# A graph-attention layer and a graph-convolution layer on one core: the projection by seven half-size products, the bias seeded in PSUM, layer 0's statistics split between two engines, and one written list of steps

## The chip, the core and the metric

One NeuronCore of a Trainium2 chip runs one program. TensorE (PE) multiplies into PSUM; VectorE (DVE), ScalarE (ACT) and GpSimd (POOL) work on rows of 128 partitions; SyncE (SP) issues most transfers, and POOL issues those whose row numbers come from a table in SBUF. Each engine takes its instructions in their written order and waits on semaphores of the others. The metric is the device time of one execution in microseconds (us); lower is better. One run of this kernel differs from another by about 0.3% (2322.24 to 2328.84 us in three runs).

## The reference

The input x has 32 batches of 512 channels by 1024 nodes; adj is 512 by 512.

```
layer 0:  q = wq . x[b],  k = wk . x[b]            (one number a node)
          scores[m, n] = leaky(q[n] + k[m]),  att = softmax over n
          agg = x[b] att^T,  out = relu(adj agg + bm)
          x = layernorm(x + out)                   (over the 1024 nodes)
layer 1:  W = adj * adj,  out[m, f] = sum_n W[n, m] x[n, f] + bias[f]
          x = layernorm(x + out)
```

The kernel never builds the 1024 by 1024 attention matrix. The score depends on q[n] + k[m] alone, so with the nodes sorted by q the softmax sums become prefix sums. Both kernels project first, z = adj x, together with q, k and a column of ones (514 columns a node), put these rows in order of q, make tables of prefix sums, and take for each node three rows of a table.

## The kernel before

**Roles.** Four batches are in work at a time. In "slot" s of the main part (`slot`, s = 1 to 29) batch s is in layer 0's end and layer 1, `mid` = s+1 has its tables made and its rows fetched, `new` = s+2 is projected and ranked, and `old` = s-1 is normalised and stored. `begin` and `opening` fill this pipeline and `end` empties it. `tc.manual_schedule()` keeps every engine's instructions in the order in which the Python code issues them, so the order of work is the order of the calls in `slot` and `phase`.

**Projection of `new`** (`project`, L266 to L282): for each of 8 groups of 128 nodes, 4 channel blocks by 2 halves of the 514 columns, 64 matmuls of 128x257 in fp32. The trace shows two MATMUL records for one fp32 matmul. `keep` (L260) copies a group's PSUM tile to `zrow` on ACT.

**Ranking of `new`.** `spread` transposes q into every partition (`qb`), `place` (L324, DVE, 1024 elements) counts for each node how many q are smaller, `send` (L338, POOL, an indirect transfer) writes the node's row of `zrow` to that place of a DRAM table `td` (two such tables alternate), and after the eighth `send` `fetch` (L377, SP, eight transfers) reads the sorted rows back into `zs`: its first six bring blocks 8, 0, 1 and 7 (424 rows of 2056 bytes), the last two the rest.

**Tables of `mid`, one slot later.** `weigh` (L395) makes the factors `lq` for four of the nine blocks of `zs` (part 0) and for the others (part 1): Exp on ACT, products on DVE. `table` (L424) runs nine steps; each is four matmuls, a copy out on ACT, a carried row copied by POOL and one by ACT, and two stores of rows to `td`. `pick` (L450, POOL, indirect) then fetches three table rows for each node, eight transfers of 128 x 6168 bytes.

**Batch s.** `shares`, `scale` and `gain` weight and add the three rows. `turn` transposes into PSUM and ACT writes relu(. + bm) into y. `add` adds x (DVE). Layer 0's statistics are `stats` (two bn_stats and one bn_aggr a row block, DVE), `root` (POOL), `shift` (DVE) and `apply` (ACT). Layer 1 is already a product by seven half-size products: `sums` makes T1 to T4 (eight half rows of 128x512), `layer1`'s `make` multiplies, 28 matmuls of 128x512, and `read` (L613 to L617) adds the seven products up from PSUM on DVE, 18 reads of 128x512, the first ones onto a bias held in SBUF. `phase` writes the order of the last 26 us of a slot: reads, places, sends and picks alternate, and `fetch(new)` is followed on POOL's queue by one more pick.

PSUM has eight banks: three two-bank tiles rotate under the tag "mm", one under "t".

Of the kernel before, what the change touches and what calls it, by code (L numbers as in the profile page):

```python
# [23 lines left out]
def gat_gcn_resnorm_kernel(  # L24
# [11 lines left out]

# [8 lines left out]
    ZW = C + 2  # L79
    G = P // 2  # L80
# [8 lines left out]
    xpool = ctx.enter_context(tc.tile_pool(name="xpool", bufs=12))  # L89
    tpool = ctx.enter_context(tc.tile_pool(name="tpool", bufs=3))  # L90
    ypool = ctx.enter_context(tc.tile_pool(name="ypool", bufs=4))
    vpool = ctx.enter_context(tc.tile_pool(name="vpool", bufs=4))
    junk = ctx.enter_context(tc.tile_pool(name="junk", bufs=1))
    small = ctx.enter_context(tc.tile_pool(name="small", bufs=3))
    single = ctx.enter_context(tc.tile_pool(name="single", bufs=1))
    ps_mm = ctx.enter_context(tc.tile_pool(name="ps_mm", bufs=3, space=bass.MemoryType.PSUM))
    ps_t = ctx.enter_context(tc.tile_pool(name="ps_t", bufs=1, space=bass.MemoryType.PSUM))
# [11 lines left out]
    vec = const.tile([3 * CT, P], F32, name="vec")  # L109
# [4 lines left out]
    bm_sb = const.tile([P, CT], F32, name="bm_sb")  # L114
    bias_bc = const.tile([P, N], F32, name="bias_bc")


# [34 lines left out]
    zs = const.tile([P, NB, ZW], F32, name="zs")  # L152
# [6 lines left out]
    xs = {}  # L159
    kept = {}  # L160

    def load(b, ct):
        xt = xpool.tile([P, N], F32, name=f"x_{b}_{ct}", tag="x")
        nc.sync.dma_start(out=xt, in_=x[b, ct * P : (ct + 1) * P, :])
        xs.setdefault(b, []).append(xt)

    for b in range(3):
        for ct in range(CT):
            load(b, ct)
        if b == 0:  # L170
            nc.sync.dma_start(out=bias_bc, in_=bias.partition_broadcast(P))
# [4 lines left out]
    for td in tdb:  # L176
        nc.sync.dma_start(
            out=td.rearrange("(s u) c -> s u c", u=3)[N:NS, 0, :], in_=zs[P + N - NS : P, 0, :]
        )
        odd = td.rearrange("(s w u) c -> s w (u c)", w=2, u=3)  # L180
        for r in range(0, NS // 2, P):
            n = min(P, NS // 2 - r)
            nc.sync.dma_start(
                out=odd[r : r + n, 1, ZW : 3 * ZW],
                in_=zs[0:n, 0:2, :].rearrange("p j c -> p (j c)"),
            )


    wmT = const.tile([P, CT, ZW], F32, name="wmT")
    w1 = adj_sb  # L190

    def turn_weights():
        pt = ps_t.tile([P, N], F32, name="pt_v", tag="t")
        nc.tensor.transpose(pt[:, 0 : 3 * CT], vec, ident[0 : 3 * CT, 0 : 3 * CT])
        nc.vector.tensor_copy(wmT[:, :, 0], pt[:, 0:CT])
        nc.vector.tensor_copy(wmT[:, :, C + 1], pt[:, CT : 2 * CT])
        nc.vector.tensor_copy(bm_sb, pt[:, 2 * CT : 3 * CT])
        for ct in range(CT):
            pt = ps_mm.tile([P, C], F32, name=f"pt_{ct}", tag="mm")
            for ot in range(CT):  # L200
                nc.tensor.transpose(
                    pt[:, ot * P : (ot + 1) * P], adj_sb[:, ot, ct * P : (ct + 1) * P], ident
                )
            if ct % 2:
                nc.scalar.copy(wmT[:, ct, 1 : C + 1], pt)
            else:
                nc.vector.tensor_copy(wmT[:, ct, 1 : C + 1], pt)
# [7 lines left out]
    def square_weights():  # L215


        nc.vector.tensor_tensor(w1, adj_sb, adj_sb, ALU.mult)
        for ct in range(CT):
            nc.vector.tensor_tensor(  # L220
                w1[:, ct, ct * P : (ct + 1) * P], w1[:, ct, ct * P : (ct + 1) * P], ident, ALU.add
            )
# [4 lines left out]
        nc.vector.tensor_tensor(bias_bc[:, hi], bias_bc[:, hi], bias_bc[:, lo], ALU.subtract)  # L227
# [11 lines left out]
    room = {  # L239
        ("T1", 0): (5, 2), ("T2", 0): (5, 0), ("T2", 1): (5, 1),  # L240
        ("T1", 1): (6, 0), ("T3", 1): (6, 2), ("T3", 0): (6, 1),
        ("T4", 0): (7, 0), ("T4", 1): (7, 2),
    }

    info = {}
    ys = {}
    vs = {}
    ranks = {}
    due = {}
    us = {}  # L250
    ops = {}
    zps = {}
    tabs = {}
    tds = {}
    mixes = {}
    bws = {}
    qbs = {}
    tops = {}

    def keep(b, nt):  # L260

        nc.scalar.copy(  # L262
            zrow[:, nt, :].rearrange("p (h c) -> p h c", h=2), zps.pop((b, nt))[:, :, 0:CE]
        )

    def project(b, nt, part, kept=True):  # L266

        xb = xs[b]
        if part == 0:
            zps[b, nt] = ps_mm.tile([P, 2, H], F32, name=f"zp_{b}_{nt}", tag="mm")  # L270
        zp = zps[b, nt]
        for ct in range(part * CT // 2, (part + 1) * CT // 2):
            for h in range(2):
                nc.tensor.matmul(  # L274
                    zp[:, h, 0:CE],
                    xb[ct][:, nt * P : (nt + 1) * P],
                    wmT[:, ct, h * CE : (h + 1) * CE],
                    start=(ct == 0),
                    stop=(ct == CT - 1),
                )  # L280
        if part == 1 and kept:
            keep(b, nt)  # L282

    def peak(b):
# [3 lines left out]
        kc = small.tile([P, NT], F32, name=f"kc_{b}", tag="kc")  # L288
        nc.vector.tensor_copy(kc, zrow[:, :, C + 1])
        nc.vector.memset(zrow[:, :, C + 1], 1.0)  # L290
        info[b] = kc

    def spread(b, to="lq"):

        pool, tag = (ps_mm, "mm") if to == "v" else (ps_t, "t")
        qb = pool.tile([P, N], F32, name=f"qb_{b}", tag=tag)
# [4 lines left out]
        mx = ps_mm.tile([P, N], F32, name=f"mx_{b}", tag="mm")  # L301
        nc.tensor.transpose(mx[:, 0:P], tops.pop(b).to_broadcast([P, P]), ident)
        qmax = small.tile([P, 1], F32, name=f"qmax_{b}", tag="qmax")
        bw = small.tile([P, 2], F32, name=f"bw_{b}", tag="bw")
        nc.vector.tensor_reduce(qmax, mx[:, 0:P], AX.X, ALU.max)
        nc.vector.tensor_scalar(bw, nel, qmax, None, ALU.mult)
        if to == "v":
            qs = vpool.tile([P, N], F32, name=f"qs_{b}", tag="v")
            nc.scalar.copy(qs, qb)
            qb = qs  # L310
        else:
            qs = lq[:, 0:N]
            nc.scalar.copy(qs, qb)
        td = tdb[b % 2]
        rank = single.tile([P, NT], F32, name=f"rank_{b}", tag="rank")
        ranki = single.tile([P, NT], U32, name=f"ranki_{b}", tag="ranki")
        sgn = single.tile([P, NT], F32, name=f"sgn_{b}", tag="sgn")
        ranks[b] = (rank, ranki)
        tds[b] = td
        bws[b] = bw  # L320
        info[b] = (qs, info[b], sgn, qmax)
        qbs[b] = qb

    def place(b, *some):  # L324

        rank, ranki = ranks[b]
        qs = qbs[b]
        for nt in some:
            o = N - P - nt * P
            lt = junk.tile([P, N], I8, name=f"lt_{b}_{nt}", tag="lt")  # L330
            nc.vector.scalar_tensor_tensor(  # L331
                lt, qs, zrow[:, nt, 0:1], first[:, o : o + N],
                ALU.subtract, ALU.is_lt, accum_out=rank[:, nt : nt + 1],
            )
        n0, n1 = some[0], some[-1] + 1
        nc.vector.tensor_scalar(ranki[:, n0:n1], rank[:, n0:n1], 3.0, None, ALU.mult)  # L336
# [723 lines left out]
```

## Time and profile before

| what | value |
|---|---|
| median of 3 runs | 2324.92 us (2322.24, 2328.84, 2324.92) |
| span of the profiled execution | 2323.5 us; the page gives no time outside it |
| mean granted TensorE clock | 0.978 |
| busy PE / DVE / ACT / POOL | 2206.9 / 2003.3 / 1403.0 / 1042.8 us |
| from 0 to the first slot | 184.56 us |
| 29 slots | 1997.34 us, 68.87 us each |
| after the last slot | 141.60 us |
| moved by DMA | 548.68 MB |

How to read it: the span is that of one execution. A group row gives the line, the engine, the operation, out<-in, shape and count, then the total busy time, the mean of one instruction in ns, and the idle time before. A timeline row begins with start and length in us; a bracket at its end is the idle time before it and who ended it. Where rows run back to back their lengths overlap, so that the distance of starts, not the length, is the cost of one in a stream.

### The profile page before, as it was taken

What the parts mean: (1) busy time and instruction counts of PE and PEld (TensorE: products, weight loads), DVE (VectorE), ACT (ScalarE), POOL (GpSimd) and SP (SyncE); (2) the same over time, 40 slices, a digit from 0 to 9 for tenths busy, and PEclk for the clock granted to TensorE, in tenths of its full rate; (3) what the DMA queues carried; (4) which work ended last, traced back from release to release, by engine and by line L of the source; (5) the groups of instructions that cost most, each with busy time, mean ns of one, the idle gap of its engine ahead of it and who ended that gap; (6) DMA issues with size and microseconds to landing.
All of it is one profiled execution on the core that took longest, in us unless ns stands there. A gap on an engine that the chain in (4) does not pass through costs nothing.

```text
span 2323.5 us, 30952 instructions
## 1 busy us (share of the span) xinstructions
PE 2206.9 (95%) x9521; PEld 1388.3 (60%) x9521; DVE 2003.3 (86%) x4153; ACT 1403.0 (60%) x2185; POOL 1042.8 (45%) x1296
## 2 busy tenths in 40 slices
PE   8969999999999999999999999999999999999775
PEld 7636666566665656666656665656666665666332
DVE  4278989888998988899988898998899888889777
ACT  2665566666556667566667556666656666755543
POOL 2424444544444544444453444454444454444433
PEclk9979999999999999999999999999999999999877
DMA  6657878777878777787877787877777877777741
GB/s 250 200 165 238 261 239 280 245 222 235 252 242 265 257 230 231 241 263 248 270 238 220 239 257 240 274 257 224 227 248 253 260 257 231 227 239 248 235 164 73
DMA packets 175421, 548.68 MB, mean 236 GB/s; under 512 B 24748, under 2 KB 24760, under 8 KB 175256
## 3 DMA queue, kind: packets, MB, share of 16 engines
q1 hardware_dynamic: 117888, 277.18, 40.3%
q0 software_dynamic: 57344, 269.52, 33.2%
q8 instruction: 76, 1.25, 0.2%
q14 instruction: 89, 0.73, 0.1%
q10 hardware_dynamic: 24, 0.01, 0.0%
HBM read 338.17 MB, written 208.43 MB: 235 GB/s over the span
## 4 chain that ended last, share of the span: by engine, by line
DVE 42%; DMA 19%; PE 16%; issue 7%; POOL 6%; ACT 6%; SPq 2%; POOLq 0%; DVEq 0%; ACTq 0%
DVE lt L331 12%; DVE v L617 9%; DMA zs<-td 8%; PE zp L274 8%; DVE st L515 6%; PE tp L431 5%; DMA td<-zrow,ranki 5%; DMA rows<-td,idx 4%; DVE rows L589 4%; DVE rows L506 3%; DVE y L553 2%; POOL td L341 2%; PE op L544 2%; DMA td<-ts 2%; SPq L389 2%
## 5 line engine op out<-in xcount | busy, mean ns | idle before, releaser
L274 PE MATMUL zp<-wmT,x 128*128 128x257 f32 x4096 | 947.7, 383 | 1.4 <-ACT zrow L262 1.3
L274 PEld LDWEIGHTS zp<-wmT,x 128*128 128x128 f32 x4096 | 757.5, 190 | 163.4 <-issue 36.8
L440 POOL COPY zs<-ts 1x513 f32<-1x513 f32 x251 | 191.2, 762 | 676.3 <-ACT ts L436 675.3
L431 PE MATMUL tp<-zs,lq 128*64 128x257 f32 x2304 | 333.2, 404 | 63.5 <-DVE lq L411 24.8
L506 DVE SCALAR_TENSOR_TENSOR rows<-rows,ra 128x512 f32<-128x512 f32 x512 | 379.4, 762 | 11.7 <-ACT rows L498 2.5
L452 POOL DMA_INDIRECT rows<-td,idx x256 | 291.9, 1140 | 204.0 <-issue 115.8
L341 POOL DMA_INDIRECT td<-zrow,ranki x256 | 279.0, 1090 | 119.7 <-DVE ranki L336 46.6
L331 DVE SCALAR_TENSOR_TENSOR lt<-qb,zrow,first 128x1024 int8<-128x1024 f32 x240 | 307.1, 1280 | 4.3
L474 ACT ACTIVATE ac<-s 128x4 f32<-128x4 f32 x64 | 13.3, 208 | 486.4 <-DVE s L473 387.9
L431 PEld LDWEIGHTS tp<-zs,lq 128*64 128x64 f32 x2304 | 153.3, 140 | 224.6 <-POOL zs L440 82.5
L356 ACT ACTIVATE sg<-lq,kc 128x1024 int8<-128x1024 f32 x240 | 275.1, 1146 | 6.8
L605 PE MATMUL oA<-y,adj_sb 128*128 128x512 f32 x512 | 243.8, 609 | 11.0 <-ACT y L536 9.9
L436 ACT COPY ts<-tp 128x514 f32<-128x514 f32 x288 | 168.4, 585 | 110.5 <-PE tp L431 85.5
L605 PE MATMUL oS<-rows,ws 128*128 128x512 f32 x480 | 210.9, 591 | 0.0
L498 ACT ACTIVATE rows<-rows,ra 128x512 f32<-128x512 f32 x256 | 166.8, 711 | 55.7 <-DVE ra L485 50.2
L262 ACT COPY zrow<-zp 128x514 f32<-128x514 f32 x256 | 144.8, 577 | 84.1 <-PE zp L274 76.6
L523 POOL TENSOR_SCALAR rs<-mv 128x1 f32<-128x1 f32 x256 | 88.6, 346 | 237.7 <-DVE mv L517 140.6
L553 DVE TENSOR_TENSOR y<-y,x 128x1024 f32<-128x1024 f32 x128 | 156.1, 1219 | 45.1 <-ACT y L548 45.1
L536 ACT ACTIVATE y<-y,nb,rs 128x1024 f32<-128x1024 f32 x128 | 158.5, 1238 | 54.5 <-DVE nb L530 53.2
L524 POOL TENSOR_TENSOR rs<-rs,mhalf 128x1 f32<-128x1 f32 x256 | 180.4, 705 | 21.4
L515 DVE BATCH_NORM_STATS2 st<-y 128x6 f32<-128x512 f32 x256 | 163.8, 681 | 2.7 <-issue 0.2
L605 PEld LDWEIGHTS oA<-y,adj_sb 128*128 128x128 f32 x512 | 94.1, 195 | 120.5 <-issue 98.1
(119 smaller groups left out, 2640.5 us busy)
## 6 DMA issues: line engine op xcount, KB each, us to landing
x<-in_x_dram SPq DMA_DIRECT2D x128, 512.0 KB
out_dram<-v SPq DMA_DIRECT2D x126, 512.0 KB
td<-ts SPq DMA_DIRECT2D x512, 120.5 KB
zs<-td SPq DMA_DIRECT2D x64, 602.3 KB
zs<-td SPq DMA_DIRECT2D x64, 240.9 KB
zs<-td SPq DMA_DIRECT2D x96, 120.5 KB
td<-ts SPq DMA_DIRECT2D x64, 96.4 KB
td<-zs SPq DMA_DIRECT2D x8, 514.0 KB
```

The source lines that it names most:

```text
L274: nc.tensor.matmul(zp[:, h, 0:CE], xb[ct][:, nt * P : (nt + 1) * P], wmT[:, ct, h * CE : (h + 1) * CE], start=(ct == 0), stop=(ct == CT - 1),)
L331: nc.vector.scalar_tensor_tensor(lt, qs, zrow[:, nt, 0:1], first[:, o : o + N], ALU.subtract, ALU.is_lt, accum_out=rank[:, nt : nt + 1],)
L341: sc = nc.gpsimd.indirect_dma_start(out=td[:, :], out_offset=bass.IndirectOffsetOnAxis(ap=ranki[:, nt : nt + 1], axis=0), in_=zrow[:, nt, ...
L356: nc.scalar.activation(sg, qs, AF.Sign, bias=kc[:, nt : nt + 1], accum_out=sgn[:, nt : nt + 1])
L431: nc.tensor.matmul(tp[i * G : (i + 1) * G, h, 0:CE], lw[:, ks[i], :], zs[:, j, h * CE : (h + 1) * CE], start=True, stop=True,)
L440: by.tensor_copy(zs[0:1, to, 1:ZW], ts[0:1, 1:ZW])
L452: nc.gpsimd.indirect_dma_start(out=rows[:, mt, :], out_offset=None, in_=tds[b].rearrange("(s u) c -> s (u c)", u=3), in_offset=bass.Indire ...
L506: nc.vector.scalar_tensor_tensor(u, g[:, k, i, 1 : C + 1], ra[:, k, i : i + 1], u, ALU.mult, ALU.add)
L515: nc.vector.bn_stats(st[:, h, :], t[:, h * H : (h + 1) * H])
L553: nc.vector.tensor_tensor(t, t, xs[b][ot], ALU.add)
L605: nc.tensor.matmul(ops[b, w][:, m, :], quarters[w][:, a, m * P : (m + 1) * P], part(y, a), start=(a == 0), stop=(a == CT // 2 - 1),)
L617: by.tensor_tensor(vs[b, mt][:, half], x0, x1, ALU.add)
```

## The change

The kernel is largely rewritten; what a batch computes is the same.

- **Projection by seven products.** Nodes by channels by columns are split in halves; four sums of quarters of x (`mix`, DVE, 128x512 each) are made for each of two groups of node blocks. 14 pairs of half products, 56 matmuls of 128x257, run into three PSUM tiles of fixed name A, B, C. Partial results are read in the middle of an accumulation (`keep`): eight copies of 128x514 on ACT and six additions of 128x514 on DVE.
- **Layer 1.** The bias is written into PSUM by `seed` before the products (four bf16 matmuls of 128x512 with a matrix of ones, the bias as three bf16 parts). The products accumulate in PSUM; four reads of 128x1024 are copies on ACT and three are additions on DVE. T1 to T4 are four subtractions of 128x1024. `SC` = 32 scales W and with it layer 1's sum.
- **Layer 0's statistics.** ACT's relu is gone: `add` takes max(PSUM, -bm) + x in one DVE instruction and takes the row's sum along. `square` makes the mean (ACT, one column) and a pass of Square with a sum (ACT, 1024), `root0` the root (POOL), `finish` the shift and the scaled row (ACT).
- **Layer 1's normalisation** (`apply`) is on ACT for all four row blocks; two were on DVE.
- **Tables.** `zs` is one column wider, later steps write their table rows into `zs` itself.
- **The order** is one string `SLOT` of step names, run once per slot. Each name has a role: `p` (project), `k` (keep), `x` (mix), `r` (place), `sd` (send), `fe` (fetch), `c` (count), `pi` (pick), `wx`/`wb` (the two halves of weigh), `t`/`e`/`cp`/`ca`/`ts` (table matmuls, copy, carries, store), `u` (turn), `ad`, `sq`, `rt`, `y` (layer 0's statistics), `sA`/`sB` (seed), `m` (products), `rd` (reads).

```diff
-        for ct in range(part * CT // 2, (part + 1) * CT // 2):
-            for h in range(2):
-                nc.tensor.matmul(zp[:, h, 0:CE], xb[ct][:, nt * P : (nt + 1) * P],
-                    wmT[:, ct, h * CE : (h + 1) * CE], start=(ct == 0), stop=(ct == CT - 1))
...
+    def mix(b, g, i, by=nc.vector):
+        of, op, more = {
+            1: ("A21", ALU.add, "A22"), 2: ("S1", ALU.subtract, "A11"),
+            3: ("A11", ALU.subtract, "A21"), 4: ("A12", ALU.subtract, "S2"),
+        }[i]
+        by.tensor_tensor(side(b, g, f"S{i}"), side(b, g, of), side(b, g, more), op)
...
+        for c in range(2):
+            nc.tensor.matmul(zp[:, m, 0:CE], side(b, g, a)[:, c, m * P : (m + 1) * P],
+                wb[:, w, c, :], start=first and c == 0, stop=c == 1, skip_group_check=not first)
...
-        nc.scalar.activation(t, op, AF.Relu, bias=bm_sb[:, ot : ot + 1])
-        nc.vector.tensor_tensor(t, t, xs[b][ot], ALU.add)
+        nc.vector.scalar_tensor_tensor(yall[:, ot], tops.pop((b, ot)), nbm[:, ot : ot + 1],
+            xs[b][:, ot], ALU.max, ALU.add, accum_out=sm)
...
+        nc.scalar.activation(xs[b][:, ot], yall[:, ot], AF.Square, bias=nm, accum_out=sq)
...
+            nc.tensor.matmul(o[:, m, :], ones.to_broadcast([P, P]), seeds[:, "AB".index(at), :],
+                start=True, stop=True)
...
+    SLOT = """
+    st1 p5 ga1 ro1 p0 st0 p3 p2 gb1 ga0 p4 k0p1 p1 ga2 gb0 p7 k011 wx0 p6 x11 p12 wb0 k0u2 st2 t0
+    gb2 p10 e0 st3 k0p5 p11 cp0 ts0 ca0 ro0 p9 k022 x12 t1 ro2 oa1 p14 ox1 e1 no1 wx1 p15 cp1 ts1
...
+    mx ca7 cp7 ts7 qb mr k121 rt3 sq2 t8 r0 sA e8 en rt2 sB r1 y1 m0 ts8 ld2 r2 sd1 y2 sd0 m1 T1 ql
+    y3 pi0 r3 m3 pi1 rdp1 r4 c0 pi3 m6 T2 sd2 r5 m2 pi2 r6 m5 rdp5 T3 m4 r7 m7 T4 rdu2 c1 pi6 m9 x01
+    c2 sd4 x02 rd11 m8 sd7 sx c3 sd6 m10 rd22 sd3 oa0 m11 sd5 ox0 c4 no0 pi5 c5 m13 x04 pi4 rd12 sc1
+    pi7 m12 c6 fe x03 rd21 sc0 sc3 c7 sc2
+    """
```

In `begin`, `whole(b)` runs a batch's projection: it issues the batch's eight mixes first, then the 14 pairs. For batch 1 the call stands behind batch 0's eight places and behind `seed_bias`, which splits the bias into its bf16 parts on DVE.

## The prediction

> **What bounds the kernel now.** First the busy times by stage: one middle slot, and all 29.
>
> ```profile
> core 0: us, PE busy (x) PEld busy (x) DVE busy (x) ACT busy (x) POOL busy (x), PEclk, DMA share, GB/s
> 1010.08:1078.09 68.01, 67.70 (x298) 42.81 (x297) 62.19 (x130) 43.51 (x68) 32.33 (x41) 1.00 0.78 250
> ...
> 184.56:2181.90 1997.34, 1969.58 (x8614) 1240.87 (x8613) 1804.40 (x3742) 1262.57 (x1972) 933.47 (x1159) 1.00 0.77 245
> ```
>
> PE is busy 67.9 of 68.87 us a slot, at full clock; DVE has 62.2, ACT 43.5. So PE's own work is the time, and about 1 us a slot is waiting. The list of waits says where; the groups give PE's prices.
>
> ```profile
> PE tp L431 <- DVE lq L411: 24.8, 24, 8.5
> PE tp L431 <- POOL zs L440: 23.3, 37, 3.0
> ...
> L274 PE MATMUL zp<-wmT,x 128*128 128x257 f32 x4096 | 947.7, 383 | 1.4 <-ACT zrow L262 1.3
> L544 PE MATMUL op<-ident,rows 128*128 128x128 f32 x1024 | 147.8, 289 | 14.5 <-DVE rows L506 14.5
> L605 PE MATMUL oS<-rows,ws 128*128 128x512 f32 x480 | 210.9, 591 | 0.0
> ```
>
> What PE waits for is the first table step: its factors, made from the fetched rows. That chain starts at PE itself, when q has been transposed (`qb`), and comes back one slot later. The timelines of PE, POOL, SP and ACT show it once:
>
> ```profile
> 1051.37 1.09 PE L298 MATMUL qb<-ident,zrow 128*128 128x128 f32 x8
> ...
> 1059.25 1.15 POOL L452 DMA_INDIRECT rows<-td,idx  x1 [4.32 <-issue]
> ...
> 1079.38 0.99 POOL L341 DMA_INDIRECT td<-zrow,ranki  x1 [0.31 <-issue]
> 1080.68 1.05 POOL L452 DMA_INDIRECT rows<-td,idx  x1 [0.31 <-issue]
> ...
> 1085.69 0.69 SPq L384 DMA_DIRECT2D zs<-td  x2
> ...
> 1091.89 0.67 ACT L403 ACTIVATE w<-zs,bw,el 128x2 f32<-128x2 f32 x2 [0.53 <-DMA zs<-td]
> ```
>
> From the end of `qb` (1052.4): last send issued at +27.0, fetch issued at +33.3, factors begun at +39.5, first table step at +41.7. PE has some 40 us of other work in between, so the chain just fits.
>
> **PE's part.** 2048 projection matmuls become 1792 (counted in the built order of both): 512 records fewer at 947.7/4096 = 0.231 us, 3.7 us a batch off the path. The four seeds are one record of 512 columns each, a kind the trace does not show: at least a 128-column record (147.8/1024 = 0.14, 0.6 a slot), at most an fp32 record of 512 (210.9/480 = 0.44, 1.8 a slot). I take 1.8, the row with the same columns. PE's slot: 67.9 - 3.7 + 1.8 = 66.0. If nothing else changed, this were the gain: 2.9 us in 29 slots, 83 us. (The Trainium skill, "TensorE: Matmul & The Clock Gate", section "Back-to-back issue gap", gives N/2.4 + 2.5 ns for a bf16 matmul, 0.216 us here, by which the seeds would be 0.9 and the slot 65.1.)
>
> **DVE and ACT**, a slot, all beside PE while they keep up. DVE: layer 0's statistics go (8 x 0.64 bn_stats, 4 x 0.21, 4 x 0.26: -6.9); 18 reads at 0.64 become three of 1024 at 1.28 (-7.8); two applies at 0.81 go (-1.6); T1 to T4 stay (-0.3); `add` becomes the form of a place (1.28 + 0.08 for 1.22: +0.6); eight mixes and six keeps come at about 0.62 (+8.7). 62.2 becomes 54.9. ACT: relu goes (-4.4); four Square at 1.24 and 0.19 for the sum (+5.7); eight one-column steps at 0.2 (+1.6); four reads at 1.0, the row of the 1024-element copy from PSUM (+4.0); two applies more (+2.4). 43.5 becomes 52.8. Neither is the bound by its sum, but ACT stands in front of more of PE's steps: PE may add to A only after ACT has read it, and the list leaves one or two projection steps (0.9 us each) as cover for a 0.58 us copy. I put all these small waits, with those of the table steps, at 1.3 us a slot instead of about 0.9 now; uncovered, each of the eight copies would cost up to 0.8.
>
> **The chain.** PE's work from `qb` to the first table step gets shorter: t8 1.0, seeds 1.8, products 24.6 (the stretch from 1052.5 to 1078.1 less t8), then only nine projection steps of four records, 8.3: together 35.7 us, where the old order has 40. So the fetch must be 4 us earlier, and the list tries that: sends first, five picks between them, three picks (pi5, pi4, pi7) behind the last send. By rows:
>
> 1. First send: highest, two places with the scaled index (1055.05 to 1057.87 for such a pair): +3.2. The second at +4.6, the first pick at +6.0 (1.4 apart: 16 issues from 1059.25 to 1081.73); its data flow from +7.8 (issue at 1059.25, queue 0 moves from 1061).
> 2. From there the queue is full. It moved 8.42 MB from 1061 to 1087, 0.324 MB a us, which makes a pick (128 x 6168 bytes) 2.44 us and a send (263 KB) 0.81. Five picks and six sends are 17.1: the last send has landed at +24.9. POOL's own issue is done at +22.9 and does not set it. The fetch is issued 1.1 later (as 1085.69 after the same sum for the old order, 1084.6): +26.0, 7 us earlier than now.
> 3. The fetch's first six transfers took 6.2 us here, with only one pick behind the sends, nearly drained. Three picks are 2.4 MB still to be moved. What that does, the opening shows, where `fetch(1)` runs beside eight picks: the fetch's issue, the factors, and the packets in 99 to 127 us.
>
> ```profile
> 97.33 0.66 SPq L384 DMA_DIRECT2D zs<-td  x2
> ...
> 110.56 0.67 ACT L403 ACTIVATE w<-zs,bw,el 128x2 f32<-128x2 f32 x2 [6.52 <-DMA zs<-td]
> ...
> q0 software_dynamic: 1130, 6.25, 70.8%
> q1 hardware_dynamic: 1172, 2.18, 28.5%
> ```
>
> Packet for packet the two queues take turns, but a pick's is three times as large: the fetch gets a quarter of the bytes, 42 packets a us for 112 alone (1237 in 1087 to 1098), and took 13.2 us to the factors. With three picks the turns last until these are gone: 0.65 MB before the fetch's first packet (+26.9), the other 1.72 MB at 0.223 a us (6.25 MB in 28 us), 7.7 us, in which the fetch gets 323 of its 424 rows; the rest is 0.9, and the landing 1.5. That is 11.0; the ends are 6.2 (no slowing) and 13.2 (slowed to the end). Some of the sends' backlog may be shorter, so I take 10.7: factors begun at +36.7. ACT (0.67) and the first product on DVE (0.3) with their hand-overs make 1.2: first table step at +37.9, where PE would be ready at +35.7.
>
> The Trainium skill speaks against this order too: "DMA: Bandwidth & Descriptors", section "Queues, rings and completion order", says that each engine goes round its queues packet by packet. The row above agrees (1130 against 1172 packets).
>
> So PE waits 2.2 us at t0. Queued behind: all of PE; on ACT, wx0 stands in front of k0u2, e0 and the scales; on DVE, wb0 in front of st2, gb2 and the mixes. Slot: 37.9 + (66.0 - 35.7) + 1.3 = 69.5, 0.6 more than 68.87. With the ends of the fetch's time it is 67.3 (no wait) to 72.0.
>
> **Begin and end.** Batch 1's projection now stands behind DVE. PE can do four steps, then needs the first sum of `mix`, which is written after eight places (42.28 to 53.34 in the trace, 11.1 us), `seed_bias` (0.6; three casts and three one-row copies, at 0.7 to 1.2 and about 0.6, the nearest rows being a copy at 0.69 for 512 and 1.22 for a 1024 subtraction; two subtractions at 1.2: 7 in all) and 0.6 for the mix: some 19 us after `qb`, less 3.6 of PE's work, where PE now goes on without a gap (41.21 to 65.72). That is 15 late, less the 3.4 saved in this batch: +12, with 3 to 18 as bounds, as the fetch of batch 1 and all behind it move along. In the end statistics lose a hop for each row block: -3, bounds -8 and +5.
>
> **Sum.** Span 2323.5 + 29 x 0.6 + 12 - 3 = 2350. The span lies 1.4 below the median of the runs, which I leave out.
>
> **The rivals.**
> - *The fetch is not slowed* (0.30). If picks and fetch share better than in the opening, the factors are ready before PE: 26.0 + 6.2 + 1.2 = 33.4. The slot is 66.0 + 1.3, less 0.6 for half of the seeds' uncertainty: 66.7, and the time 2323.5 - 63 + 9 = 2270. For it: the 6.2 of the steady slots. Against it: 13.2 in the only place where picks run behind. It decides where the fetch takes under 8.5 us.
> - *ACT sets the second half* (0.08). From t0 to the next `qb` ACT has some 27 us of work in 30.3 of PE's, in one line with the table's copies: 0.3 more at each of eight steps makes a slot of 71.9 and a time of 2420. Against it: ACT's waits now are long, DVE takes less.
> - *Fewer products are not fewer on the chip* is out: the built order shows 1792.
>
> **Chances.** The forecast's case has 0.62. Its own range, with 9.0 to 13.2 us for the fetch (slots of 67.8 to 72.0), is 2302 to 2424; of it 0.10 is faster, 0.08 no change, 0.44 slower. Faster by over 0.3% (what a measurement here can tell): 0.10 + 0.30 = 0.40; within it 0.08; slower 0.44 + 0.08 = 0.52. The range of 2255 to 2408 leaves out the upper end of the forecast's case and half of the ACT case, and little below.
>
> **What would show it.** Right: first table steps that wait 1 to 4 us for the factors in nearly every slot; fetch issued about 26 after `qb`, factors 10 to 12 later; q1 at a quarter of the bytes in that stretch; a PE gap of over 10 us near 45. Wrong: factors 6 to 7 us after the fetch (then near 2270), or the waits at other PE steps. A wait much longer than the forecast would also show half clock in the rows after it: the 4.43 us wait at 111 us was followed by a table step of 1.82 instead of 1.09.

## The result, and the profile after

| | before | after |
|---|---|---|
| median (lowest to highest) | 2325.79 us (2322.24 to 2328.84), 4 runs | 2512.32 us (2509.39 to 2517.91), 4 runs |
| ratio | | 1.0811, 95% interval 1.0783 to 1.0839 |
| span of the profiled execution | 2323.5 us | 2509.4 us |
| mean granted TensorE clock | 0.978 | 0.932 |
| from 0 to the first slot | 184.56 us | 217.17 us |
| a slot (mean of 28) | 68.89 us | 74.35 us |
| last slot and end | 210.0 us | 210.3 us |

The change costs 186 us: 28 slots at 5.46 make 153, the opening 32.6, the rest nothing. The busy times by stage (the row of the 28 slots, the columns as in the rows shown of before):

```profile
core 0: us, PE busy (x) PEld busy (x) DVE busy (x) ACT busy (x) POOL busy (x), PEclk, DMA share, GB/s
217.17:2299.09 2081.92, 1879.33 (x7954) 1175.50 (x7980) 1560.69 (x3081) 1425.63 (x2408) 811.44 (x1120) 0.95 0.73 228
```

Divided by 28 slots: PE is busy for 67.1 of 74.35 us, where before it was 67.9 of 68.9. DVE has 55.7, ACT 50.9. No engine is full any more, and the clock in the slots is 0.95 instead of 1.00. The list of waits (us in total, times, longest) and the page's group of the table steps say where PE stands:

```profile
ACT w L449 <- DMA zs<-td: 265.7, 29, 10.6
DVE lq L461 <- ACT w L449: 236.4, 33, 14.1
PE tp L483 <- DVE lq L461: 198.6, 30, 8.0
PE oA L646 <- ACT y L599: 19.7, 33, 1.7
...
L483 PE MATMUL tp<-zs,lq 128*64 128x257 f32 x2304 | 361.8, 432 | 241.9 <-DVE lq L461 198.6
```

In the slots PE has one long wait each, at the first table step, 6.6 us on average, ended by the factors, which are ended by the fetch. The timelines of PE, POOL, SP and ACT for one slot, in order of time:

```profile
1077.20 1.04 PE L349 MATMUL qb<-ident,zrow 128*128 128x128 f32 x8
1079.18 0.39 PE L629 MATMUL oA<-seeds,ones 128*128 128x512 bf16 x1
1079.63 0.59 PE L629 MATMUL oB<-seeds,ones 128*128 128x512 bf16 x2
1081.53 1.13 POOL L388 DMA_INDIRECT td<-zrow,ranki  x1 [0.94 <-DVE ranki L381]
1101.34 0.97 POOL L388 DMA_INDIRECT td<-zrow,ranki  x1 [0.30 <-issue]
1105.28 0.99 POOL L516 DMA_INDIRECT rows<-td,idx  x1 [0.30 <-issue]
1105.77 0.66 SPq L434 DMA_DIRECT2D zs<-td  x2
1118.59 0.67 ACT L449 ACTIVATE w<-zs,bw,el 128x2 f32<-128x2 f32 x2 [9.02 <-DMA zs<-td]
1119.36 2.25 PE L483 MATMUL tp<-zs,lq 128*64 128x257 f32 x8 [6.47 <-DVE lq L461]
1121.54 3.78 PE L311 MATMUL zp_A<-wb,y 128*128 128x257 f32 x8
```

Last send at 1101.34, the three late picks behind it, the fetch at 1105.77, and the factors 12.8 us later. Then the second loss: the table step takes 2.25 and the next eight records 3.78, about twice what the same rows take after no wait (1.09 and 1.90 to 2.00). The granted clock around it (columns as in the row above), from PE's last work before the wait to 20 us behind it:

```profile
1111.53:1114.94 3.41, 1.35 (x7) 0.84 (x5) 0.21 (x1) 0.00 (x0) 0.00 (x0) 1.00 0.97 259
1114.94:1125.18 10.24, 5.82 (x17) 4.23 (x18) 4.00 (x9) 2.83 (x6) 2.13 (x5) 0.50 0.69 154
1125.18:1146.00 20.82, 20.82 (x121) 15.04 (x119) 17.97 (x36) 18.11 (x30) 5.52 (x9) 1.00 0.41 128
```

The clock is halved from 2.1 us after PE's last row until just behind the eight records. DMA queues from 1105.8 to 1108.8, from 1108.8 to 1113.3 and from 1113.3 to 1118 us (packets, MB, share):

```profile
q0 software_dynamic: 178, 1.01, 97.9%
...
q0 software_dynamic: 195, 1.03, 65.6%
q1 hardware_dynamic: 221, 0.40, 31.2%
...
q1 hardware_dynamic: 554, 1.02, 96.3%
```

Queue 0 carries the picks, queue 1 the fetch. For 3 us after its issue the fetch moves next to nothing, then it gets 28% of the bytes, then nearly all.

### The profile page after: what moved, and what is told of

Its sections match the earlier page's. It is cut to its first block, busy times and chain, and to the rows that moved or that the text cites. A ratio compares the mean times of both kernels' runs of the same rounds, so it can differ in the third digit from the quotient of the medians.

```text
span 2509.4 us, 30414 instructions
## 1 busy us (share of the span) xinstructions
PE 2180.2 (87%) x9105; PEld 1356.9 (54%) x9137; DVE 1808.9 (72%) x3574; ACT 1635.0 (65%) x2758; POOL 935.2 (37%) x1293
## 3 DMA queue, kind: packets, MB, share of 16 engines
q1 hardware_dynamic: 121216, 277.05, 38.5%
## 4 chain that ended last, share of the span: by engine, by line
PE 49%; DMA 18%; ACT 10%; issue 6%; DVE 4%; POOL 4%; SPq 3%; POOLq 0%; ACTq 0%; DVEq 0%
PE zp_A L311 13%; DMA zs<-td 12%; PE tp L483 10%; PE oA L646 7%; PE zp_B L311 5%; PE op L567 5%; DMA td<-zrow,ranki 4%; PE oC L646 4%; PE oB L646 4%; ACT x L583 3%; POOL td L388 3%; SPq L439 2%; ACT y L599 2%; DVE y L574 2%; ACT zs L495 1%
## 5 line engine op out<-in xcount | busy, mean ns | idle before, releaser
L646 PE MATMUL oA<-y,adj_sb 128*128 128x512 f32 x768 | 356.4, 600 | 21.3 <-ACT y L599 19.7
L376 DVE SCALAR_TENSOR_TENSOR junk<-qb,zrow,first 128x1024 int8<-128x1024 f32 x240 | 306.6, 1277 | 26.0 <-ACT lq L368 12.5
L401 ACT ACTIVATE junk<-lq,kc 128x1024 int8<-128x1024 f32 x240 | 274.0, 1141 | 2.0
L311 PE MATMUL zp_A<-wb,x 128*128 128x257 f32 x1024 | 264.6, 392 | 1.6 <-DVE zrow L330 1.6
L574 DVE SCALAR_TENSOR_TENSOR y<-op,nbm,x 128x1024 f32<-128x1024 f32 x128 | 164.0, 1284 | 88.3 <-PE op L567 88.3
L311 PEld LDWEIGHTS zp_A<-wb,x 128*128 128x128 f32 x1024 | 186.5, 191 | 59.8 <-issue 12.4
L449 ACT ACTIVATE w<-zs,bw,el 128x7 f32<-128x7 f32 (+1 forms) x128 | 43.2, 386 | 265.8 <-DMA zs<-td 265.7
L599 ACT ACTIVATE y<-y,nb,r 128x1024 f32<-128x1024 f32 x128 | 158.8, 1240 | 4.3
L311 PE MATMUL zp_A<-wb,y 128*128 128x257 f32 x512 | 160.4, 467 | 0.7 <-ACT zrow L332 0.7
L675 DVE BATCH_NORM_STATS2 st<-v 128x6 f32<-128x512 f32 x240 | 153.4, 681 | 0.0
L583 ACT ACTIVATE x<-y,nm 128x1024 f32<-128x1024 f32 x128 | 147.1, 1149 | 4.1
```

Source lines behind the costliest of these rows:

```text
L311: nc.tensor.matmul(zp[:, m, 0:CE], side(b, g, a)[:, c, m * P : (m + 1) * P], wb[:, w, c, :], start=first and c == 0, stop=c == 1, skip_gro ...
L376: nc.vector.scalar_tensor_tensor(junk(b)[:, 0:N], qbs[b], zrow[:, nt, 0:1], first[:, o : o + N], ALU.subtract, ALU.is_lt, accum_out=rank[: ...
L401: nc.scalar.activation(junk(b)[:, N : 2 * N], qs[b], AF.Sign, bias=kcs[b][:, nt : nt + 1], accum_out=signs(b)[:, nt : nt + 1],)
L574: nc.vector.scalar_tensor_tensor(yall[:, ot], tops.pop((b, ot)), nbm[:, ot : ot + 1], xs[b][:, ot], ALU.max, ALU.add, accum_out=sm,)
L583: nc.scalar.activation(xs[b][:, ot], yall[:, ot], AF.Square, bias=nm, accum_out=sq)
L599: nc.scalar.activation(yall[:, ot], yall[:, ot], AF.Identity, bias=nb, scale=r)
```

## The experiments

Theory: the factors come late because the picks behind the last send share the DMA engines with the fetch, and the lower clock follows from PE's wait. Rivals: the fetch is slow by itself; the chain of table steps sets the time; DVE or ACT bound the slot. The table gives means over the slots of each trace, in us from the end of `qb`, PE's idle time a slot, and the time (median where there were several runs). Kernels with an r leave picks out. Those with an interval in the text ran four or five times, the others once. In the edits, `...` leaves steps out, and the last argument of `run` names steps that a slot skips.

| kernel | fetch issued | factors begun | first table step | next qb | PE idle | slot | time |
|---|---|---|---|---|---|---|---|
| before | 33.7 | 40.3 | 42.0 | 68.9 | 1.0 | 68.9 | 2325.8 |
| after | 27.3 | 40.7 | 41.4 | 74.5 | 7.2 | 74.35 | 2512.3 |
| no late picks (r) | 27.4 | 33.9 | 34.9 | 65.8 | 1.0 | 66.1 | 2272.5 |
| two late picks (r) | 27.2 | 38.5 | 39.2 | 71.8 | 5.2 | 71.9 | 2437.5 |
| picks ahead of sends | 31.3 | 37.8 | 38.6 | 71.7 | 4.5 | 71.6 | 2431.6 |
| picks behind tables | 27.4 | 33.7 | 34.6 | 77.1 | 7.1 | 77.1 | 2590.3 |
| filled wait | 27.3 | 40.6 | 41.4 | 73.0 | 2.9 | 72.9 | 2468.1 |
| tables later | 27.3 | 42.8 | 44.6 | 71.2 | 4.7 | 71.2 | 2433.8 |
| both orders | 31.4 | 37.9 | 39.1 | 72.1 | 5.5 | 72.1 | 2444.9 |
| order by engines | 37.0 | 43.2 | 44.0 | 73.5 | 5.4 | 73.4 | 2485.0 |
| order by waits | 31.7 | 38.2 | 39.1 | 69.5 | 3.0 | 69.5 | 2362.5 |
| passes in gaps | 32.0 | 38.5 | 39.7 | 69.0 | 2.7 | 69.0 | 2345.5 |
| second pass first | 33.2 | 39.6 | 40.4 | 70.4 | 3.2 | 70.3 | 2382.5 |
| root behind sends | 32.7 | 39.1 | 39.9 | 69.3 | 2.9 | 69.3 | 2351.3 |

### No late picks, and one less

```diff
-        run(s, SLOT, ("pi4", "pi5", "pi6", "pi7") if s == B - 3 else ())
+        run(s, SLOT, ("pi4", "pi5", "pi7") + (("pi6",) if s == B - 3 else ()))
```

> Leaves out, in every slot, the three picks that stand behind the last send on POOL's queue (pi4, pi5, pi7); the rows that they would bring are older data, every other instruction is unchanged. Theory (the picks share the DMA engines with the fetch, packet for packet, and that alone makes the factors late): from the fetch's issue to the first factors 6.5 us instead of 13.4, so factors near 34 us after qb; no PE wait at the first table step (6.6 us a slot in the changed kernel) and no half-clock rows after it (some 2 to 2.8 us); slots of 74.35 - 6.6 - 2 = 66 to 68 us, 29 x 67 + 217 + 136 = 2296 us in all (2270 to 2330). Rival (the fetch is slow by itself, by the new pitch of zs or because the sends land late): factors still 12 to 14 us behind the fetch, 2490 to 2515 us. Rival (ScalarE or VectorE sets the slot once the wait is gone): no wait, but slots of 70 us or more, 2380 us and up.

2272.5 us. The same slot from SP, ACT and PE:

```profile
1016.29 0.66 SPq L434 DMA_DIRECT2D zs<-td  x2
1022.44 0.67 ACT L449 ACTIVATE w<-zs,bw,el 128x2 f32<-128x2 f32 x2 [2.35 <-DMA zs<-td]
1023.34 1.23 PE L483 MATMUL tp<-zs,lq 128*64 128x257 f32 x8
1024.50 2.01 PE L311 MATMUL zp_A<-wb,y 128*128 128x257 f32 x8
```

6.2 us from fetch to factors, no wait in the PE row, and full clock behind it. The picks alone make the factors late; the new shape of `zs` does not, and neither ACT nor DVE bounds this slot. With only pi7 left out (`("pi7",)` in the same place):

> Leaves out only the last of the three late picks (pi7) in every slot; its rows are older data, everything else is as in the changed kernel. Theory (each late pick costs the fetch the time that its bytes take on the shared engines): with none of the three the factors came 6.4 us behind the fetch, with all three 13.4, so with two near 11; PE's wait at the first table step 4 to 4.5 us, slots of 71.5 to 73 us, 2430 to 2470 us. Rival (any pick in front of the fetch holds it for as long, since the queue's start is what is late): factors 12.5 us or more behind the fetch, slots of 73.5 us and up, 2490 us or more.

11.2 us from fetch to factors, slots of 71.9: with none, two and three late picks it is 6.4, 11.2 and 13.4, so the second and third late pick cost the fetch 2.1 to 2.4 us each (one alone was not run), near the 2.44 that the forecast took for a pick's bytes.

### Picks ahead of the sends, picks behind the tables

```diff
-    y3 pi0 ... m7 T4 rdu2 c1 pi6 m9 ... sd5 ox0 c4 no0 pi5 c5 m13 x04 pi4 rd12 sc1 pi7 m12 c6 fe
+    y3 pi0 ... m7 T4 rdu2 c1 pi4 pi7 pi5 pi6 m9 ... sd5 ox0 c4 no0 c5 m13 x04 rd12 sc1 m12 c6 fe
```

> Only the order of POOL's queue in the slot is changed: the three picks that stood behind the last send (pi4, pi5, pi7) are listed ahead of the last five sends, as the kernel before had them; nothing is left out. Theory (what counts up to the factors is the bytes that the sixteen DMA engines have to move, in whatever order): the fetch is issued later, near 31 us after qb instead of 27.3, and runs undisturbed, 6.5 to 8 us to the factors: factors at 37.5 to 40.5, the PE wait at the first table step 3 to 6 us, slots of 71 to 74.3 us, 2410 to 2510 us. Rival (it is the order alone that costs, the fetch should just not be shared): factors at 34 to 35 us as in the run without these picks, no wait, slots of 66 us, 2280 us.

The fetch comes 4.1 us later and takes 6.5 instead of 13.4: the factors are 2.8 us earlier, the slot 2.7 shorter. The theory's ranges held. Issuing the fetch earlier at the price of picks behind it bought nothing. But the factors still come 3.9 us after PE could use them.

```diff
+    for nt in (4, 5, 7): also(0, f"pj{nt}", lambda b, nt: do(b, f"pi{nt}"), nt)
...
-    ... pi5 c5 m13 x04 pi4 rd12 sc1 pi7 ...
+    ... p14 e1 wx1 p15 cp1 pj4 pj5 pj7 ts1 ... t4 av3 x13 oa1 ox1 no1 ...
```

> The three picks are kept but issued one slot step later, on POOL behind the second carry of the table chain, so that they move while PE runs tables and projection; the normalizers, scales, gains and turns of the rows that they bring are listed later accordingly (first turn some 3 us later). Theory (three picks out of the stretch between qb and the factors are worth what leaving them out was worth, since the DMA engines have room later in the slot): factors near 34 us, no wait at the first table step, slots of 66 to 69 us: 217 + 29 x 67.5 + 136 = 2310 us (2270 to 2370), all work done. Rival (the rows come too late for the gains and turns, which then set the time, or the rest of the fetch is shared instead and the third table step waits): a new wait of 3 us or more at the turns or at a table step, slots of 70 us and up, 2390 us or more.

The rival was right: 2590.3 us, the slowest of all. The factors come at 33.7 and the first table step waits for nothing, but the rows now come late for what uses them (waits of this kernel):

```profile
PE op L567 <- DVE rows L560: 96.8, 92, 5.6
...
DVE s L531 <- DMA rows<-td,idx: 89.3, 31, 4.9
```

DVE's normalizers wait for the rows, PE's turns for the gains, and the rows of `table` and `turn` behind these waits run at half clock (eight turns in 1.97 us instead of 1.09).

### The wait filled

```diff
+        for i in range(10 if step == 0 and b > 1 else 0):
+            nc.tensor.matmul(tp[:, 0, 0:CE], ident, wb[:, 0, 0, :], start=True, stop=True)
```

> Adds ten products of 128x257 (4.35 us at full clock by the rows of L311) on constants into the first table step's bank ahead of it, in each slot, where PE otherwise waits 6.6 us; their result is overwritten. Theory (PE's wait itself lowers the clock of what follows: a first table step of 2.25 instead of 1.09 and four half-products of 3.5 to 3.8 us instead of 1.9): with a remaining wait of about 2.3 us these rows stay at full clock, and the slot becomes shorter by 2 to 3 us although work is added: slots of 71.5 to 72.5, 2430 to 2460 us, clock 0.97 instead of 0.93. Rival (the lower clock follows from something else than PE's idleness, or half the rows would wait anyway): no change or longer by what a filled wait overshoots, 2505 to 2540 us.

2468.1 us: 44 us less with 4.35 us of PE work more in each slot. PE's timeline:

```profile
1025.88 4.50 PE L481 MATMUL tp<-wb,ident 128*128 128x257 f32 x20
1031.65 1.36 PE L485 MATMUL tp<-zs,lq 128*64 128x257 f32 x8 [1.28 <-DVE lq L461]
1032.94 2.00 PE L311 MATMUL zp_A<-wb,y 128*128 128x257 f32 x8
```

The first table step comes at 41.4 as before; from there to `qb` 33.0 became 31.6. So the wait itself costs clock. The gain, 1.4 a slot, is under the expected 2 to 3: in 18 of 28 slots all rows behind the wait ran at full clock (slots of 71.4 to 72.9), in the other ten a wait of 2.2 to 4.3 us was left and some rows behind it ran at half clock (73.8 to 77.8).

### The tables later

```diff
-    ... p7 k011 wx0 p6 x11 p12 wb0 k0u2 st2 t0 gb2 p10 e0 st3 k0p5 p11 cp0 ts0 ca0 ...
+    ... p19 ga3 sf3 sc6 wx0 p8 ga5 wb0 ga6 p18 t0 sc7 sf2 ga7 k1p1 av2 k012 p22 e0 cp0 ca0 ts0 ...
```

> Only the order of the slot's list is changed: the steps of the table chain (factors, tables, table copies, carries, table stores) are listed later, so that nine more half-products (0.52 us each, 4.7 us) run before the first table step on PE, and ScalarE and VectorE have their own work (keeps, sums, normalizers, scales) ahead of the factors; the three picks stay behind the last send. Theory (the factors come 40.7 us after qb whatever stands ahead of them; the changed kernel loses time because its list reaches the first table step at 34.5): PE's wait there falls from 6.6 us to 1.5 to 3, the rows after it run at full clock, from the first table step to the next qb 33 becomes 26 to 28 us; slots of 67 to 69 us, 217 + 29 x 68 + 136 = 2325 us (2290 to 2370). Rival (the table chain's own length, each step waiting for a copy and a carry, sets the time from the first step to qb): that time stays 31 to 33, slots of 73 to 75, 2470 to 2520 us. Rival (the picks): as the theory, but it would say nothing of why the factors are late; factors stay 13 us behind the fetch here and 6.5 us in the run without the picks.

2433.8 us (ratio 1.0481, interval 1.0438 to 1.0524; the trace is of the fastest of four runs, 2416.7). The expectation had a wrong price in it: a half-product step is four records, 0.87 us by the rows of L311, not 0.52, so 7.8 us went ahead of the first table step, too much. That step now comes at 44.6, with the clock at 0.974. From there to `qb` it is 26.6 as expected. The gain, 79 us, is less than half of the expected 187. Most slots are the same to 0.1 us (70.7), which speaks for the list, and not a transfer, as what sets them.

Both orders together, the picks ahead of the sends and four half-products ahead of the tables:

```diff
-    ... p7 k011 wx0 p6 x11 p12 wb0 k0u2 st2 t0 gb2 p10 e0 st3 k0p5 p11 cp0 ts0 ca0 ro0 p9 k022 x12 t1 ...
+    ... p7 k011 p6 x11 p12 k0u2 st2 gb2 p10 st3 k0p5 p11 ro0 p9 k022 x12 wx0 ro2 p14 wb0 t0 oa1 ox1 e0 ...
```

> Only the slot's list is changed, in two places: the three picks stand ahead of the last five sends (as in the run with the picks ahead), and four half-products more (0.87 us each by the rows of L311, 3.5 us) run before the first table step, with the later tables spread over the rest, no work left out. Theory: the fetch is issued near 31 us after qb and the factors come at 37.8 as in that run; PE reaches the first table step at 34.7 + 3.5 = 38.2 instead of 34.7, so the wait of 3.9 us falls below 1 and nothing runs at half clock; from there to the next qb 27.5 to 28.5 us: slots of 66 to 67.5, 217 + 29 x 66.8 + 136 = 2290 us (2270 to 2325), below the kernel before. Rival (the table chain's copies and carries, or the second part of the fetch, which landed at 46.5, hold PE later): waits of 2 us or more at later table steps, slots of 69 to 71, 2350 to 2410 us.

2444.9 us (1.0536, 1.0515 to 1.0558), slower than either side had it. Fetch and factors came as expected (31.4, 37.9) and the wait at the first table step went, but PE waits elsewhere: 0.8 us a slot at table steps, which the rival named, and 3.2 at projection steps, which it did not (PE's timeline):

```profile
1022.97 1.14 PE L311 MATMUL zp_A<-wb,x 128*128 128x257 f32 x4 [0.68 <-ACT zrow L332]
1028.29 1.14 PE L311 MATMUL zp_A<-wb,rows 128*128 128x257 f32 x4 [1.23 <-ACT zrow L332]
1034.07 0.44 PE L567 MATMUL op<-ident,rows 128*128 128x128 f32 x2 [0.86 <-DVE rows L560]
1037.51 1.14 PE L311 MATMUL zp_A<-wb,rows 128*128 128x257 f32 x4 [0.93 <-ACT zrow L332]
```

PE may not add to A before ACT has copied it, and these copies stood behind ACT's scales and passes: the loss of cover that the forecast had priced at up to 0.8 a copy.

### Order or load

Five kernels move only steps in the list, with the picks ahead and no work left out (the first against both orders), to see if what remains is order or the load of ACT and DVE. All but the first have the later sums of the opening too (below).

```diff
-    ... k0u2 st2 gb2 p10 st3 k0p5 p11 ro0 p9 k022 x12 wx0 ... r1 y1 m0 ts8 ld2 ...
+    ... k011 k0p5 oa1 ox1 p6 x11 no1 p12 k0u2 sc4 sc5 p10 ... sc7 wx0 ... r1 y1 ld3 av3 so3 m0 ts8 ld2 ...
```

> Again only the slot's list: as the run with both orders, but ScalarE's and VectorE's steps are put in the order in which that run's PE waits asked for them (normalizers and scales of the second half ahead of the factors, where ScalarE had 5 us free; each copy that frees a bank of PE ahead of scales and final passes; the layer norm's statistics and passes of the batch before behind the tables). Theory (with the picks ahead and the first table step moved, what is left of the loss are 3.2 us of PE waits for copies out of its banks, 0.8 at table steps and 0.8 at the turns, all of them matters of order): these fall to 1 to 2 us, slots of 67 to 69.5 us, 2300 to 2370 us. Rival (the loss is VectorE's and ScalarE's load, so it goes to other rows): slots stay at 71 to 73 us, 2410 to 2450 us.

A miss, 2485.0: PE's waits at projection steps fell from 3.2 to 1.4, but the last table store (`ts8`) stood on SP's queue behind an output store (`so3`) that waits for ACT. The first pick stood 5.1 us, and the fetch came at 37.0. The next one, against both orders:

```diff
-    ... k0u2 st2 gb2 p10 st3 k0p5 ... p15 sc4 ro3 p13 k021 ... p18 sc7 sf2 ga7 k1p1 ... p23 av1 ... k1u2 p16 ...
+    ... k0u2 oa1 ox1 gb2 no1 p10 k0p5 sc4 ... p15 k021 sc6 p13 st2 ... p18 k1p1 sc7 ... p23 k1u2 st3 ...
```

> The run with both orders and the opening's later sums, with only those steps of the slot's list moved that its waits name: the copies that free PE's banks (k021, k1p1, k1u2) go ahead of scales and final passes, normalizers and first scales of the second half ahead of the factors, two of the statistics behind the second table step; the list's part behind the projection, with the table stores and the sends, stays as it was (in the last run a table store stood behind an output store, the sends started at 3.4 us and the fetch at 37.0 instead of 31.4). Theory (order, not load): PE waits for copies 3.2 to 1 us, table steps and turns 1.6 to 1, factors at 37.9, slots of 68 to 70 us, 208.5 + 29 x 69 + 136 = 2345 us (2310 to 2375). Rival (load of ScalarE and VectorE): slots 71 to 73 us, 2405 to 2450 us.

2362.5 us (1.0171, 1.0144 to 1.0197), as the theory had it: with the copies `k021 k1p1 k1u2` ahead of the scales PE's waits at projection steps are gone, and the slot is 2.6 shorter with the same work. Then the final passes in the gaps, against this one:

```diff
-    ... wb1 k111 p17 t2 gb6 ga7 gb7 e2 cp2 ca2 ts2 av1 p23 ... p21 rt1 sq3 t7 k112 sh p26 e7 ...
+    ... p19 av1 t1 ... wx1 av0 k012 ... k1u2 sf2 av2 ... p21 rt1 t7 k112 sh p26 e7 pk mx ca7 cp7 ts7 sq3 ...
```

> The run ordered by waits, with ScalarE's four final passes (L699, 1.24 us each) moved forward into the places where it waited 1.5 to 2 us for the first table steps, and the last square pass behind the copy of the table step before qb. Theory (PE's remaining waits of 0.8 us at qb and 0.8 at the second product are ScalarE's last steps of the slot, order again): both fall by half or more, slots of 67.5 to 68.7 us, 210 + 28 x 68.2 + 204 = 2324 us (2305 to 2345), at the level of the kernel before. Rival (load): slots of 69 to 70 us, 2350 to 2370 us.

2345.5 us (1.0103, 1.0088 to 1.0118), the fastest with all work done. Half of the theory held: the wait at `qb` (0.8) went, but the one at the second product grew from 0.7 to 1.4, so that the time is just past the theory's upper end and the slot, 69.0, is the rival's. The last two, against this one:

```diff
-    ... ts7 sq3 ld3 qb mr k121 rt3 sq2 t8 r0 sA e8 en rt2 sB r1 y1 m0 ts8 ld2 r2 sd1 y2 sd0 m1 T1 ql y3
+    ... ts7 y1 qb mr k121 sq2 t8 r0 sA e8 rt2 en sq3 sB r1 m0 ts8 ld2 ld3 r2 sd1 rt3 y2 sd0 m1 T1 ql y3
...
+    ... ts7 sq3 ld3 qb mr k121 rt3 y1 t8 r0 sA e8 en sB sq2 r1 m0 ts8 ld2 r2 sd1 y3 sd0 m1 T1 rt2 ql y2
```

> As the last run, with the second finishing pass of layer 0 (y1, ScalarE, which the second product waits for) ahead of qb's last copies, the two last squares behind it, and one of their two roots behind the first send. Theory (order): the 1.44 us of PE wait at the second product fall below 0.4, sends start at 2 to 2.5 us instead of 3.0, slots of 67 to 68 us, 209 + 28 x 67.6 + 203 = 2305 us (2290 to 2325), below the kernel before by up to 1%. Rival (ScalarE's later passes or POOL's roots take it back, at the third pair of products or at the sends): slots of 68.5 to 70 us, 2335 to 2375 us.

2382.5 us (1.0240, 1.0223 to 1.0257), the rival's case and past its range. That product's wait is 0.02, but a root that waits for a late square stands on POOL ahead of the sends (POOL's timeline):

```profile
1025.95 0.22 POOL L590 TENSOR_SCALAR r<-sq 128x1 f32<-128x1 f32 x1 [3.52 <-ACT x L583]
1026.26 0.57 POOL L591 TENSOR_TENSOR r<-r,mhalf 128x1 f32<-128x1 f32 x1
1027.12 1.11 POOL L388 DMA_INDIRECT td<-zrow,ranki  x1 [0.30 <-issue]
```

The fetch and the factors come 1.1 us later, and PE's wait at table steps grew by 1.8.

> Between the last two runs: the second finishing pass goes ahead of the last square only (the third square stays ahead of qb's copies), and the root of the last square goes behind both first sends on POOL. Theory (in the last run the product's wait of 1.44 us went, but roots that waited for late squares held POOL's sends, the fetch came at 33.2 instead of 32.0 and PE waited 2.5 us at the first table step again): sends from 2.0 us, fetch near 31.6, factors near 38.1, PE's wait at the second product below 0.6 and at the first table step below 0.7: slots of 67.5 to 68.5 us, 209 + 28 x 68 + 204 = 2317 us (2300 to 2335), level with the kernel before or just below. Rival (the later third finishing pass holds the products that need it, or the ranks): slots of 69 us and up, 2345 us or more.

2351.3 us (1.0121, 1.0100 to 1.0142), the rival's case once more: PE waits 1.3 us for the late finishing pass (y2) instead.

### The opening

```diff
         do(0, "mx mr ql en")
+        do(1, "x01 x02 x04 x03 x11 x12 x14 x13")
         do(0, "r0 r1 sd0 sd1 r2 r3 sd2 sd3 r4 r5 sd4 sd5 r6 r7 sd6 sd7 fe")
```

> One line in the opening: batch 1's eight operand sums (VectorE, L302) are issued right behind batch 0's line, ahead of batch 0's places and of the bias seeds, the rest unchanged. Theory (the 13.4 us PE wait at 64 us is batch 1's first sums queued on VectorE behind them): the wait goes, batch 0's sends start some 5 us later, the first slot starts 8 to 13 us earlier, the slots stay at 74.3 us: 2499 to 2505 us. Rival (the rank chain is next in line and takes the time back, since its places are now behind eight sums of 0.7 us): the first slot starts within 3 us of 217, 2510 us.

The rival was right: first slot at 219.8 (2534.9 us in all, its slots 0.7 longer, which the edit does not touch and these runs do not explain). The 13.4 us wait split in two, and ACT and PE show what was next:

```profile
59.40 0.59 ACT L332 COPY zrow<-zp_A 128x514 f32<-128x514 f32 x1 [17.05 <-DVE ranki L381]
60.04 3.79 PE L311 MATMUL zp_A<-wb,y 128*128 128x257 f32 x8 [6.45 <-ACT zrow L332]
```

Batch 1's copies go to the same `zrow` that batch 0's ranks are still read from.

```diff
+        if b == 2:
+            for f in before[0]:
+                f()
         do(b, "x01 x02 x04 x03 x11 x12 x14 x13")
```

> Only the opening: batch 2's eight operand sums (VectorE, 8 x 0.69 us) are issued behind batch 1's first places, sends and batch 0's third table step instead of ahead of them. Theory (the 10.1 us PE wait at 103.6 us of the changed kernel is a carry on POOL behind four sends, whose places stand on VectorE behind these sums): that wait falls by 4 to 6 us, and the first slot starts 3 to 6 us earlier than at 217; slots unchanged, 2504 to 2508 us in a profile like the changed kernel's. Rival (another step of the opening is late next, as with batch 1's sums): the first slot starts within 2 us of 217.

The first slot starts at 208.3, 8.9 us earlier (3 to 6 were expected); the 10.1 us wait is 4.45, as expected. In all 2510.0, since this trace's slots are 0.3 longer (74.69). Added to other orders, the two edits did this:

> The later table chain and the early sums of batch 1 together. Theory: the two add, slots of 67 to 69 us and a first slot 8 to 13 us earlier: 2315 us (2280 to 2360), which is at the level of the kernel before the change or below it. Rival (either one's gain is taken back): within 5 us of the run with the later tables alone.

2432.6 us (1.0470, 1.0437 to 1.0503), no change by the early sums, as the rival had it.

> As the run with both orders, with batch 2's sums in the opening behind batch 0's third table step as well, which started the first slot 8.9 us earlier in its own run. Theory: the two add, 2270 to 2290 us, 6 to 10 us below the run with both orders alone. Rival (the opening's gain is given back in the slots): within 3 us of it.

2439.4 us (1.0506, 1.0483 to 1.0529), 5.5 below both orders alone and the first slot 8.1 earlier: the later sums are kept, a little below the expected 6 to 10.

## Why the prediction was wrong, step by step

It had 2350 us (2255 to 2408), and a slower kernel at 0.52. The sign, at little better than even odds, and the place of the wait were right; the size was off by 162 us against the median, beyond the range.

- **PE's part**: right in direction. The slot without late picks is 65.8 us with 0.9 of waits, so PE's work is 64.9, where the text took 66.0. The seeds cost 0.22 each, 0.88 in all, not 1.8: the bf16 row agrees with the 0.216 that the text quoted.
- **DVE and ACT**: 54.9 and 52.8 forecast, 55.7 and 50.9 measured. Neither bounds a slot.
- **The chain, steps 1 and 2**: first send +3.3 (forecast +3.2), first pick +6.5 (+6.0), POOL's last send issued at +23.2. The fetch is issued at +27.3, not +26.0: a miss of 1.3.
- **The chain, step 3**, is the term that failed: from the fetch to the factors 13.4 us, not 10.7. The text let the fetch's first packet move 0.9 us after its issue; it took 3.1, and the sharing then went on as forecast (a quarter of the bytes). This is past even the upper end, 13.2, the opening's row. That row is close by chance: there the fetch was issued ahead of the eight picks, its first packet moved 0.9 us after its issue, and it shared the engines to the end.
- **The wait**: 6.6 instead of 2.2 us. Of the 4.4, 1.3 are the later fetch and 2.7 the slower one, 0.9 comes from PE, which is ready at +34.8 instead of +35.7, and 0.4 goes back, as the hand-over takes 0.8 and not 1.2 (rounded terms). So first table step at +41.4, not +37.9.
- **What the wait does** failed too: half clock was named as a sign of a longer wait, but the sum had it at nothing, though the row at 111 us gave a price (1.82 for 1.09 after 4.43 us). The first table step takes 2.25 us instead of 1.27 in the trace without late picks, the eight records behind it 3.15 instead of 2.00: 2.1 us a slot, 60 us in all. Filling the wait showed the cause.
- Slot: 3.5 for the later first table step, 2.1 for the clock, less 0.7 for smaller waits behind it: 69.5 becomes 74.35. In 29 slots that is 141 of the 159 us between the forecast and the span; the other 18 are begin and end.
- **Begin**: +32.6 instead of +12. The gap of over 10 us was there (13.4, from 50.9), but the text saw one queue where there were three: the sums, the shared `zrow` behind them, and, 40 us later, a carry on POOL behind four sends (10.1 us), of which the later sums took 5.6 away. **End**: -5.6 instead of -3, if the last slot is as long as the others.
- **Rivals**: "the fetch is not slowed" had 2270; without late picks the kernel took 2272.5. Its condition did not hold, and its total is close by luck: with the picks out, the 29 slots were 18 us shorter than its sum, and begin and end 29 us longer than before where it had 9. "ACT sets the second half" had the wrong place at this list, but it is what the later lists met: once the factors wait no longer, ACT's copies, passes and squares do, by where they stand, not by their sum. Whether some order reaches the 66 us of the slot without late picks with all work done is open: the best here, 69.0, is 1% slower than the kernel before.

## What to carry to other kernels

Fewer instructions on the bound engine are worth something only if the step that it then reaches earlier can come earlier too: before counting a gain, look for the first instruction that waits on a transfer, and ask when its data land. A transfer that the bound engine waits for should not be issued while others are still queued on the shared DMA engines, even if it is issued earlier thereby: here it came 4.1 us later behind picks that were done, and its data 2.8 us earlier. Put a price on a wait twice, once for its length and once for the slower rows behind it, and when such a wait is gone, read the list of waits again, for the next one is a matter of order.

## What the runs showed of the hardware

**PE after a wait.** Over all 18 traces, the 98 first table steps that had waited 5 us or more (in six traces) took 2.25 to 2.26 us at a granted clock of 0.50; the 276 that had waited under 0.5 us took 1.09 to 1.44 at 0.98 to 1.00; between 2 and 4.5 us they took anything from 1.36 to 2.33. The Trainium skill, "TensorE: Matmul & The Clock Gate", section "What's actually happening", has half clock after an idle window of some 3.4 us that runs freely. The traces agree on the window, by their own records of the granted clock: between 200 and 2000 us their 175 spells of half clock last 3.41, 6.83 or 10.24 us. They differ on idle: in the window just ahead of a spell PE was busy for a share of 0 to 0.49 (1.35 of 3.41 us in the slot above), and not idle in 126 of the 175. Cut into windows of 3.41 us at these changes, the traces show 8992 full-clock windows that were followed by another, and none of these had PE busy for less than 0.41; of the 324 half-clock windows, full clock came behind all with 0.88 or more and behind none with 0.86 or less. So a wait shorter than a window can cost clock too, by where it falls.

**A queue with a head start.** With three picks queued, the fetch's first packet moved 3.1 us after its issue on average (2.3 to 3.6 over 28 slots), after some 174 packets of the other queue alone; with two queued it was 3.0, with none 1.0. After that the queues took turns, 195 packets to 221 in the slot above, as the Trainium skill, "DMA: Bandwidth & Descriptors", section "Queues, rings and completion order", has it for the packets of one engine. What holds the first packet these runs don't show.
